# Two transformer blocks on one core: stack loads behind a store, four places for two small tiles, and additions moved from GpSimd to VectorE

## The chip, the cores and the metric

The kernel runs on one NeuronCore of a Trainium2 chip. The metric is device time in microseconds (us), the median of three runs; less is better. A profile of one more execution is read beside it. The engines are called PE (TensorE), DVE (VectorE), ACT (ScalarE), POOL (GpSimd) and SP (SyncE, which here only issues DMAs).

## The reference

16 sequences of 256 tokens with 512 channels pass two blocks. Everything is float32.

```python
# block 0: cross attention to a context, then an MLP with a hidden width of 2048
x = x + mha(ln(x), ln(ctx), mask) @ proj_w + proj_b
x = x + gelu(ln(x) @ fc1_w + fc1_b) @ fc2_w + fc2_b
# block 1: causal self attention, cross attention, a small MLP
mask0 = 1 - all(x == 0)
x1 = ln1(x  + mha1(x, x, mask0, causal=True))
mask1 = 1 - all(x1 == 0)
x2 = ln2(x1 + mha2(x1, ctx, mask1))
z = relu(x2 @ fc1_w.T + fc1_b) * mask0
out = ln3(x2 + (z @ fc2_w.T + fc2_b) * mask0)

# in block 1's attention, 16 heads of 32 channels:
energy  = Q @ K.T                                # Q, K, V times the row mask
lengths = sum(energy[:, :, 0, :] != 0, axis=-1)  # of the first query's row
energy  = -inf where column >= lengths; also where column > row, if causal
out     = softmax(energy / sqrt(32)) @ V
```

## The kernel before

A matrix product in float32 is made of three passes over operands split into a high and a low part (`mm3`). The work goes by groups of two sequences (512 tokens), eight groups in all. Three stages follow one another: block 0's attention (0 to about 780 us of the span), block 0's MLP (to about 1400 us), and block 1 (`block1`). Block 1 has sixteen jobs, eight of self attention and eight of cross attention, and then a small MLP.

**Two streams in each attention.** A generator `stream` makes the attention proper: for each job eight units (two sequences by four chunks of four heads), for each unit four heads with scores (L408), exponentials (L433), transposes (L449) and the product with the values (L468). A generator `feed` makes what a job needs: queries (`project_t` with w["q"]), keys, values, and the transposed inputs of the next job (`front`, `context`). `weave` alternates the two on PE by a running count of cost. Before the first job there is nothing to weave: the first `feed` runs to its end, and only then does the stream build its first unit. PE keeps the order in which the program was written. The instructions of the other engines, and SP's DMA issues with them, are put in order by a planner: it runs a timeline with costs of its own and lets an instruction go when its inputs, its buffer and its engine are free in that timeline. So a DMA that is written late in the program can stand early in SP's queue. Every engine, SP too, then works its queue strictly in order, and an instruction that waits holds up those behind it.

**Stacks.** A chunk of queries or keys (128 rows by 512 tokens, a high and a low part) is taken out of PSUM by ACT and DVE (`split`, L132 and L133; L122 and L123 in block 0) into a tile `qk` and stored to DRAM by `keep` (L378, 512 KB). A unit's operands come back from there into one of three tiles `stack` by `build`: six DMAs of 128 KB (L389, L393), and in block 1 a small one with a row of the length mask (L398). The tile `qk` has one buffer for queries and one for keys in block 0 (`halves`), and two for each in block 1. The next chunk but one (in block 0 the next) cannot be taken out of PSUM before the store of this one has landed.

**Key counts.** For each chunk of keys `lengths` multiplies the first token's queries with the keys (L1280, into a PSUM bank of the tag "pt", of which there are two, shared with the transposes of L449). DVE adds the two parts (L1288, L1289), counts the nonzeros (L1291), makes a row of 0 or -2^100 by a comparison with the tile `cols` (L1296), and SP stores it (L1300). The tiles `lbias` and `n` have two buffers each.

**Context rows.** In cross attention, rows of the context (128 by 512) are loaded into `cx` (`context_rows`, L1435), multiplied by the row mask on POOL (`context`, L1442), transposed on PE (L277) and split. `cx` takes one of three buffers with the tag "t512", which also serve `junk` in `norm` (L1252), and `relu` and `y` in the last MLP. At the end of a job's keys, two or three rows of the next job are asked for; a fourth is asked for once the first has been used.

**Additions and norms.** When a unit is done, `finish` transposes its result (L1347), scales it on DVE into `zz` (L1349), and adds it to the residual `x` on POOL (L1356, 128x256). After every fourth unit two rows' norms are queued (`norm`, `layer_norm`): statistics and scaling on DVE (L238, L239, L241, L251, L252), and one power of -1/2 on POOL (L242).

**Masks.** `tri` (a causal mask of 0 and -2^100, 128x384) and `cols` (the numbers 0 to 255) are made once at the start. `tri` is an operand of the custom DVE instruction of L423, which adds the mask, scales, and takes the minimum in self attention.

Of the kernel before, what the change touches and what calls it, by code (L numbers as in the profile page):

```python
# [10 lines left out]
F32 = mybir.dt.float32  # L11
F32R = mybir.dt.float32r
U8 = mybir.dt.uint8
BF16 = mybir.dt.bfloat16
AF = mybir.ActivationFunctionType
ALU = mybir.AluOpType
# [4 lines left out]
P = 128  # L21
B, S, C, H = 16, 256, 512, 16
D = C // H
HID = 4 * C
KC = C // P
HPC = P // D
NB = 2
NT = S // P
G = NB * NT
N = G * P  # L30
NG = B // NB
EPS = 1e-5
SC = 1.0 / math.sqrt(D)
NEG = -(2.0**100)
# [7 lines left out]
def kernel(ctx: ExitStack, tc: tile.TileContext, a, out):  # L42
# [7 lines left out]
    nc = tc.nc  # L50

    const = ctx.enter_context(tc.tile_pool(name="const", bufs=1))
# [10 lines left out]
    nc.vector.memset(warm, 0.0)  # L63
    nc.scalar.activation(warm, warm, AF.Exp)
    nc.gpsimd.memset(nhalf, -0.5)
    cols = const.tile([P, S], F32, name="cols")
    nc.gpsimd.iota(
        cols, [[1, S]], base=0, channel_multiplier=0, allow_small_or_imprecise_dtypes=True
    )

    tri = const.tile([P, P + S], F32, name="tri")
    nc.gpsimd.memset(tri, 0.0)
    for t, at in ((0, 0), (1, P)):
        w = (t + 1) * P
        nc.gpsimd.affine_select(
            out=tri[:, at : at + w],
            in_=tri[:, at : at + w],
# [9 lines left out]
    for i in range(NB):  # L87
        own = hmask[:, i, i * HPC : (i + 1) * HPC]
        nc.gpsimd.memset(own, 1.0)
        for base, step in ((0, 1), (D - 1, -1)):  # L90
            nc.gpsimd.affine_select(
                out=own,
                in_=own,
# [261 lines left out]
    class Attention:  # L355
# [19 lines left out]
        def keep(self, job, c, slot, t):  # L375

            d = self.scratch.tile([P, 2, N], F32, tag=f"d{slot}", name=f"d{slot}")
            nc.sync.dma_start(out=d, in_=t.bitcast(F32))  # L378
            job.kept[slot, c] = d

        def build(self, job, i, c):
# [98 lines left out]
        def stream(self, jobs):  # L480
            LAG = 3
            heads = [(u, j) for u in range(len(jobs) * len(self.UNITS)) for j in range(HPC)]
            units = {}
            mixed = {}
            for n in range(len(heads) + LAG + 4):
                if n < len(heads):
                    un, j = heads[n]
                    if j == 0:
                        job = jobs[un // len(self.UNITS)]
                        if un % len(self.UNITS) == 0:  # L490
                            yield MARK
                            job.begin()
                        u = units[un] = Unit()
                        u.job = job
                        u.i, u.c = self.UNITS[un % len(self.UNITS)]
                        u.st = self.build(job, u.i, u.c)
                        u.rs = self.pool.tile([P, NT, HPC], F32, tag="rs", name="rs", bufs=3)
                        u.e, u.pt = {}, []
                    self.scores(units[un], j)
                    yield 2 * 110.0  # L500
                if LAG <= n < len(heads) + LAG:
                    un, j = heads[n - LAG]
                    yield self.turn(units[un], j)

                if n in mixed:
                    u = units.pop(mixed.pop(n))
                    yield u.job.finish(u)
                    self.done += 1
                if self.later:
                    self.later.pop(0)()  # L510
                m = n - LAG - 1
                if 0 <= m < len(heads) and heads[m][1] == HPC - 1:
                    mixed[n + 2] = heads[m][0]
                    u = units[heads[m][0]]
                    u.job.scale(u)
                    yield self.mix(u)
            while self.later:
                self.later.pop(0)()
# [4 lines left out]
    class Job:  # L523
        bias = None
# [746 lines left out]
        split_sb(own, (q0[:, :, : NB * HPC], q0[:, :, D:]))  # L1271
        return q0

    def lengths(pool, scratch, k, q0, neg):


        ps = bank("pt", "ps_e0")[: D + NB * HPC, :S]
        for i in range(NB):
            for x in range(2):
                nc.tensor.matmul(  # L1280
                    ps,
                    q0[:, i, :],
                    k[x][:, ts(i, S)],
                    start=(i == 0 and x == 0),
                    stop=(i == NB - 1 and x == 1),
                )
        bias = pool.tile([NB * HPC, S], F32, tag="lbias", name="lbias")
        nc.vector.tensor_copy(bias, ps[D:])  # L1288
        nc.vector.tensor_tensor(bias, bias, ps[: NB * HPC], ALU.add)  # L1289
        n = pool.tile([NB * HPC, 2], F32, tag="n", name="n")  # L1290
        nc.vector.tensor_scalar(  # L1291
            bias, bias, 0.0, None, ALU.not_equal, ALU.add, accum_out=n[:, 0:1]
        )
        nc.vector.reciprocal(n[:, 1:2], n[:, 0:1])
        nc.vector.tensor_scalar(n[:, 1:2], n[:, 1:2], 0.0, neg, ALU.mult, ALU.add)
        nc.vector.tensor_scalar(  # L1296
            bias, cols[: NB * HPC, :], n[:, 0:1], n[:, 1:2], ALU.is_ge, ALU.mult
        )
        d = scratch.tile([NB * HPC, S], F32, tag="dbias", name="dbias")
        nc.sync.dma_start(out=d, in_=bias)  # L1300
        return d


    def block1(mlp0):
        tables, more = {}, {}

        class Mha(Job):
# [11 lines left out]
            def norm(self, t):  # L1319
                x, table = self.x[:, t, :], tables["ln2" if self.cross else "ln1"]  # L1320
                layer_norm(pool, x, table[:, 0, :], table[:, 1, :])
                if not self.cross:
                    junk = pool.tile([P, C], F32, tag="t512", name="junk", bufs=3)
                    nonzero(junk, x, m1[:, self.g, t : t + 1])
                nc.sync.dma_start(
                    out=xd[3 if self.cross else 2][self.g][ts(t, P), :], in_=x
                )
# [16 lines left out]
            def finish(self, u):  # L1344
                pz = u.bank[:, S:].rearrange("p (t n) -> p t n", n=P)
                for t in range(NT):
                    nc.tensor.transpose(pz[:, t, :], u.zs[:, ts(t, P)], ident)  # L1347
                zz = pool.tile([P, NT, P], F32, tag="zz", name="zz")
                nc.vector.tensor_tensor(  # L1349
                    zz.rearrange("p t (j d) -> p t j d", d=D),  # L1350
                    pz.rearrange("p t (j d) -> p t j d", d=D),
                    u.rr.rearrange("p t (j o) -> p t j o", o=1).to_broadcast([P, NT, HPC, D]),
                    ALU.mult,
                )
                xv = self.x[:, u.i * NT : (u.i + 1) * NT, ts(u.c, P)]
                nc.gpsimd.tensor_tensor(out=xv, in0=xv, in1=zz, op=ALU.add)  # L1356
                self.left -= 1
                if self.left % KC == 0:
                    for t in range(u.i * NT, (u.i + 1) * NT):
                        att.later.append(lambda t=t: self.norm(t))  # L1360
                return NT * T_PASS
# [44 lines left out]
        pool = sbuf(ctx, "work3", 2)  # L1406
        scratch = ctx.enter_context(tc.tile_pool(name="scratch3", bufs=10, space=DRAM))
        att = Attention(pool, scratch, 3, True)
        tok0 = [pool.tile([P, NB, D + NB * HPC], F32R, name=f"tok{i}", bufs=1) for i in range(6)]
        for q0 in tok0:  # L1410
            nc.gpsimd.memset(q0.bitcast(F32), 0.0)

        def stage():
            return pool.tile([P, C], F32, tag="pts", name="wst", bufs=6)
# [15 lines left out]
        cxs = {}  # L1430

        def context_rows(n, t):
            if n < len(jobs) and jobs[n].cross and (n, t) not in cxs and t < G:
                cx = cxs[n, t] = pool.tile([P, C], F32, tag="t512", name="cx", bufs=3)
                nc.sync.dma_start(out=cx, in_=of("ctx", jobs[n].g)[:, t, :])  # L1435

        def context(n, t):
# [28 lines left out]
        def feed(n):  # L1466
            job = jobs[n]
# [19 lines left out]

            def count(c):
                job.bias[c] = lengths(
                    pool, scratch, ks.pop(c), q0s[c], -NEG if job.cross else NEG  # L1490
                )
                return 4 * 112.0

# [10 lines left out]
            if n == 0:  # L1504
                weight(0, "v")
            weight(n + 1, "k")
            for t in range(3 if n + 1 > NG else 2):
                context_rows(n + 1, t)
            between = [lambda: count(KC - 1), lambda: following(n, 2)]
            yield from values(pool, w["v"].w, kv, job.v, range(NT), between)  # L1510
# [17 lines left out]
        def up(g, c):  # L1528
            if c == 0:
                h_ts[g] = inputs("c_t")  # L1530
            ps = yield from project_t(w["q"].w, c, x_ts[g])
            r = pool.tile([P, N], F32, tag="t512", name="relu", bufs=3)
            nc.scalar.activation(r, ps, AF.Relu, bias=f1_b[:, c : c + 1])
            split_sb(r, (h_ts[g][0][:, c, :], h_ts[g][1][:, c, :]))

        def down(g, t):
            x = xs[g][:, t, :]
            y = pool.tile([P, C], F32, tag="t512", name="y", bufs=3)
            nc.scalar.activation(y, tables["fc2_b"], AF.Identity, scale=m0[:, g, t : t + 1])
            nc.gpsimd.tensor_tensor(out=x, in0=x, in1=y, op=ALU.add)  # L1540
            ps = yield from project(w["k"].w, h_ts[g], t)
            nc.vector.scalar_tensor_tensor(x, ps, m0[:, g, t : t + 1], x, ALU.mult, ALU.add)
            layer_norm(pool, x, tables["ln3"][:, 0, :], tables["ln3"][:, 1, :])
            nc.sync.dma_start(out=out[NB * g + t // NT, ts(t % NT, P), :], in_=x)
# [83 lines left out]
```

## Time and profile before

| | |
|---|---|
| median of 3 runs | 2765.36 us (2759.30 to 2766.42) |
| the profiled execution's own time | 2762.91 us |
| its span | 2761.2 us |
| PE busy | 2657.0 us, 96% of the span |
| DVE busy | 2051.9 us, 74% |
| ACT busy | 1821.9 us, 66% |
| POOL busy | 630.3 us, 23% |
| granted TensorE clock over the span | 0.991 of full speed |
| self attention, 1440 to 1925 us | PE 474.8 of 485.0 us busy, DVE 359.5, POOL 88.7 |
| cross attention, 1925 to 2600 us | PE 649.3 of 675.0 us busy, DVE 518.5, POOL 161.5 |
| last MLP, 2600 us to the end | PE 152.6 of 161.0 us busy |

The profile is of one execution. A line of it names the source line, the engine, the operation and the tiles, then how long it took; in square brackets stands how long the engine had been idle before it, and what released it. A wait costs time only where the engine that waits is the one that sets the end. "PEclk" is the share of TensorE's full clock that was granted.

### The profile page before, as it was taken

What the parts mean: (1) busy time and instruction counts of PE and PEld (TensorE: products, weight loads), DVE (VectorE), ACT (ScalarE), POOL (GpSimd) and SP (SyncE); (2) the same over time, 40 slices, a digit from 0 to 9 for tenths busy, and PEclk for the clock granted to TensorE, in tenths of its full rate; (3) what the DMA queues carried; (4) which work ended last, traced back from release to release, by engine and by line L of the source; (5) the groups of instructions that cost most, each with busy time, mean ns of one, the idle gap of its engine ahead of it and who ended that gap; (6) DMA issues with size and microseconds to landing.
All of it is one profiled execution on the core that took longest, in us unless ns stands there. A gap on an engine that the chain in (4) does not pass through costs nothing.

```text
span 2761.2 us, 56625 instructions
## 1 busy us (share of the span) xinstructions
PE 2657.0 (96%) x18970; PEld 2241.7 (81%) x18970; DVE 2051.9 (74%) x5947; ACT 1821.9 (66%) x5286; POOL 630.3 (23%) x696
## 2 busy tenths in 40 slices
PE   6999999999899998999989999999999999999998
PEld 5777777776899998999968777777777777777787
DVE  7766667657955569999957777777777777777887
ACT  4877777777655555444547778786777776777522
POOL 6222212113401100111211111115212221214333
PEclk9999999999999999999999999999999999999999
DMA  6655656656333344443464665667565665655321
GB/s 214 197 183 170 182 171 192 182 164 169 107 123 138 123 150 175 168 157 136 167 225 159 195 197 187 194 190 227 183 196 188 188 194 170 189 174 173 97 91 54
DMA packets 287808, 465.40 MB, mean 169 GB/s; under 512 B 36256, under 2 KB 188320, under 8 KB 279328
## 3 DMA queue, kind: packets, MB, share of 16 engines
q1 hardware_dynamic: 287520, 461.78, 52.0%
q8 instruction: 153, 2.51, 0.4%
q14 instruction: 135, 1.11, 0.1%
HBM read 284.97 MB, written 176.69 MB: 167 GB/s over the span
## 4 chain that ended last, share of the span: by engine, by line
PE 76%; DVE 10%; DMA 4%; ACT 3%; issue 3%; POOL 2%; SPq 1%; POOLq 0%; DVEq 0%; ACTq 0%
PE ps_p L258 18%; PE ps_v L258 14%; PE down L1027 9%; PE ps_pt L449 9%; PE ps_z L468 5%; PE ps_s L408 5%; PE up_sc L914 5%; PE up_pt L914 3%; PE up_mm L914 3%; PE ps_t L277 2%; DVE e L423 1%; ACT e L433 1%; DVE x L252 1%; DMA d<-qk 1%; PE ps_z L1347 1%
## 5 line engine op out<-in xcount | busy, mean ns | idle before, releaser
L433 ACT ACTIVATE e<-e,mn 128x256 f32<-128x256 f32 (+1 forms) x1024 | 487.5, 480 | 71.7 <-DVE mn L423 69.4
L455 ACT COPY pt<-ps_pt 128x512 f32<-128x512 f32 (+1 forms) x696 | 378.3, 546 | 178.5 <-PE ps_pt L449 165.5
L449 PE MATMUL ps_pt<-ident,e 128*128 128x128 f32 x2816 | 436.3, 273 | 15.4 <-DVE lbias L1289 8.8
L449 PEld LDWEIGHTS ps_pt<-ident,e 128*128 128x128 f32 x2816 | 336.3, 140 | 56.3 <-DVE lbias L1289 5.7
L408 PE MATMUL ps_s<-stack 97*128 97x256 f32 (+1 forms) x1536 | 331.8, 297 | 18.8 <-ACT e L433 12.0
L408 PEld LDWEIGHTS ps_s<-stack 97*128 97x128 f32 (+1 forms) x1536 | 269.0, 190 | 78.3 <-ACT e L433 19.2
L433 ACT ACTIVATE e<-ps_s,mn 128x256 f32<-128x256 f32 x512 | 240.9, 483 | 59.2 <-DVE mn L419 44.0
L1356 POOL TENSOR_TENSOR x<-x,zz 128x256 f32<-128x256 f32 x128 | 95.4, 745 | 737.0 <-DVE zz L1349 687.0
L1027 PE MATMUL down<-w_h,c_t 128*128 128x256 f32 x900 | 255.4, 285 | 5.6 <-DVE c_t L142 5.6
L1027 PE MATMUL down<-w_h,x_t 128*128 128x256 f32 x868 | 245.9, 283 | 4.4 <-ACT x_t L141 4.4
L423 DVE CUSTOM_DVE_ANT_0 e<-mb,ps_s 128x256 f32<-128x256 bf16 x512 | 192.7, 415 | 75.4 <-PE ps_s L408 73.8
L1027 PE MATMUL down<-w_l,x_t 128*128 128x256 f32 x868 | 246.2, 284 | 0.0
L242 POOL TENSOR_TENSOR rstd<-rstd,nhalf 128x1 f32<-128x1 f32 x192 | 142.4, 747 | 360.6 <-DVE rstd L241 358.8
L258 PE MATMUL ps_p<-x_t,q_h 128*128 128x512 f32 x640 | 215.4, 417 | 4.2 <-DVE qk L128 2.1
L419 DVE TENSOR_REDUCE mn<-ps_s 128x2 f32<-128x512 f32 x256 | 175.1, 684 | 48.7 <-PE ps_s L408 46.5
L468 PE MATMUL ps_z<-pt,v 128*32 128x256 f32 (+1 forms) x3072 | 202.2, 370 | 7.2 <-DVE pt L453 6.5
L423 DVE CUSTOM_DVE_ANT_0 e<-tri,ps_s 128x128 f32<-128x128 f32 (+1 forms) x512 | 160.2, 346 | 53.6 <-PE ps_s L408 51.3
L433 ACT ACTIVATION_READ_ACCUMULATOR e<-e,mn 128x1 f32 x1024 | 197.5, 193 | 0.0
L1027 PEld LDWEIGHTS down<-w_h,c_t 128*128 128x128 f32 x900 | 171.0, 190 | 7.8 <-DVE c_t L142 7.8
L1027 PEld LDWEIGHTS down<-w_h,x_t 128*128 128x128 f32 x868 | 166.4, 192 | 4.8 <-ACT x_t L141 4.6
L468 PEld LDWEIGHTS ps_z<-pt,v 128*32 128x32 f32 x3072 | 83.5, 109 | 105.8 <-issue 28.0
L1027 PEld LDWEIGHTS down<-w_l,x_t 128*128 128x128 f32 x868 | 165.2, 190 | 0.0
(250 smaller groups left out, 7247.8 us busy)
## 6 DMA issues: line engine op xcount, KB each, us to landing
stack<-d SPq DMA_DIRECT2D x1152, 128.0 KB
d<-qk SPq DMA_DIRECT2D x192, 512.0 KB
hid<-ho SPq DMA_DIRECT2D x32, 1024.0 KB
raw<-hid SPq DMA_DIRECT2D x32, 1024.0 KB
x<-xd SPq DMA_DIRECT2D x128, 256.0 KB
xd<-x SPq DMA_DIRECT2D x96, 256.0 KB
xin<-in_x_dram SPq DMA_DIRECT2D x32, 256.0 KB
xin<-in_ctx_dram SPq DMA_DIRECT2D x32, 256.0 KB
```

The lines of the kernel that those rows point to most:

```text
L242: nc.gpsimd.tensor_tensor(out=rstd[:, 1:2], in0=rstd[:, 0:1], in1=nhalf, op=ALU.pow)
L258: nc.tensor.matmul(ps, w[p], x[q], start=(k == 0 and i == 0), stop=(k == kc - 1 and i == 2))
L408: nc.tensor.matmul(ps[:, t, :], u.st[: self.rows, 0, j, ts(t, P)], u.st[: self.rows, 1, j, :], start=True, stop=True,)
L419: nc.vector.tensor_reduce(mn, ps, AX.X, ALU.min)
L423: nc.vector.tensor_tensor_reduce(out=e[:, at], in0=bias[t], in1=ps[:, t, : job.width[t]], scale=-SC, scalar=BIG, op0=ALU.add, op1=ALU.min, ...
L433: nc.scalar.activation(e[:, at], ps[:, t, :] if bias is None else e[:, at], AF.Exp, bias=mn[:, t : t + 1], scale=-1.0, accum_out=u.rs[:, t ...
L449: nc.tensor.transpose(pp[:, ts(x, P)], e[:, at : at + P], ident)
L455: nc.scalar.copy(pt[:, :n], pp[:, :n])
L468: nc.tensor.matmul(z[ts(j, D), w[0] * P :], job.v[u.i * NT + mc][:, u.c * P + j * D : u.c * P + (j + 1) * D], u.pt[j][:, x0 * P : (x0 + le ...
L914: nc.tensor.matmul(ps[:, mm, :], w[p][:, k, :], x[q][:, k, :], start=(first and mm == k == j == 0), stop=(k == 1 and j == 2), skip_group_c ...
L1027: nc.tensor.matmul(ps[:, t, :], x[p][:, mm, ts(t, P)], w[r][:, bo, :], start=(q == mm == t == j == 0), stop=(q == self.NS - 1 and mm == 1 ...
L1356: nc.gpsimd.tensor_tensor(out=xv, in0=xv, in1=zz, op=ALU.add)
```

## The change

It has five edits. (1) `build` of a stream's first unit, and of every later one, is queued on SP behind `first`, the last store that `keep` had issued when the stream began, which is that of the first job's last chunk of keys. Both attentions use `stream`, so this holds for block 0 too. (2) The tag "t512" has four buffers in place of three, and where three context rows of the next job were asked for at the end of the keys, four are. (3) `lbias` and `n` are one tile each over all 128 partitions, and each of a job's four chunks of keys has its own place in it, at partition 0, 32, 64 or 96, in place of two buffers in rotation. (4) In self attention the addition to `x` is made by DVE, in cross attention by POOL as before. (5) `tri` and `cols` are bfloat16, which holds their values exactly; with the smaller `lbias` this frees the SBUF space for the fourth buffer.

```diff
-    cols = const.tile([P, S], F32, name="cols")
+    cols = const.tile([P, S], BF16, name="cols")
...
-    tri = const.tile([P, P + S], F32, name="tri")
+    tri = const.tile([P, P + S], BF16, name="tri")
...
         def keep(self, job, c, slot, t):
             d = self.scratch.tile([P, 2, N], F32, tag=f"d{slot}", name=f"d{slot}")
-            nc.sync.dma_start(out=d, in_=t.bitcast(F32))
+            self.last = nc.sync.dma_start(out=d, in_=t.bitcast(F32)).ins
...
-                        u.st = self.build(job, u.i, u.c)
+                        if un == 0:
+                            first = self.last
+                        with tc.issue_after(first):
+                            u.st = self.build(job, u.i, u.c)
...
-    def lengths(pool, scratch, k, q0, neg):
+    def lengths(pool, scratch, k, q0, neg, place):
...
-        bias = pool.tile([NB * HPC, S], F32, tag="lbias", name="lbias")
+        bias, n, own_cols = (x[place * D : place * D + NB * HPC] for x in (*counts[0], cols))
         nc.vector.tensor_copy(bias, ps[D:])
         nc.vector.tensor_tensor(bias, bias, ps[: NB * HPC], ALU.add)
-        n = pool.tile([NB * HPC, 2], F32, tag="n", name="n")
...
-            bias, cols[: NB * HPC, :], n[:, 0:1], n[:, 1:2], ALU.is_ge, ALU.mult
+            bias, own_cols, n[:, 0:1], n[:, 1:2], ALU.is_ge, ALU.mult
...
+    counts = []
...
-                    junk = pool.tile([P, C], F32, tag="t512", name="junk", bufs=3)
+                    junk = pool.tile([P, C], F32, tag="t512", name="junk", bufs=4)
...
                 xv = self.x[:, u.i * NT : (u.i + 1) * NT, ts(u.c, P)]
-                nc.gpsimd.tensor_tensor(out=xv, in0=xv, in1=zz, op=ALU.add)
+
+                own = nc.gpsimd if self.cross else nc.vector
+                own.tensor_tensor(out=xv, in0=xv, in1=zz, op=ALU.add)
...
+        counts.append(
+            (pool.tile([P, S], F32, name="lbias", bufs=1), pool.tile([P, 2], F32, name="n", bufs=1))
+        )
...
-                cx = cxs[n, t] = pool.tile([P, C], F32, tag="t512", name="cx", bufs=3)
+                cx = cxs[n, t] = pool.tile([P, C], F32, tag="t512", name="cx", bufs=4)
...
                 job.bias[c] = lengths(
-                    pool, scratch, ks.pop(c), q0s[c], -NEG if job.cross else NEG
+                    pool, scratch, ks.pop(c), q0s[c], -NEG if job.cross else NEG, c
                 )
...
-            for t in range(3 if n + 1 > NG else 2):
+            for t in range(G if n + 1 > NG else 2):
                 context_rows(n + 1, t)
...
```

The tiles `relu` and `y` of the last MLP get the same fourth buffer.

More of the change, by code (lines that the diff above doesn't have):

```diff
@@ L1531, in up @@
             ps = yield from project_t(w["q"].w, c, x_ts[g])
-            r = pool.tile([P, N], F32, tag="t512", name="relu", bufs=3)
+            r = pool.tile([P, N], F32, tag="t512", name="relu", bufs=4)
             nc.scalar.activation(r, ps, AF.Relu, bias=f1_b[:, c : c + 1])
@@ L1537, in down @@
             x = xs[g][:, t, :]
-            y = pool.tile([P, C], F32, tag="t512", name="y", bufs=3)
+            y = pool.tile([P, C], F32, tag="t512", name="y", bufs=4)
             nc.scalar.activation(y, tables["fc2_b"], AF.Identity, scale=m0[:, g, t : t + 1])
```

## The prediction

> **What bounds the kernel now.** I read the page first, then the busy time in stretches of 20 us, then the timelines of PE, SP, POOL and DVE around the stretches in which PE loses time. PE is busy 96% of the span and makes most of the chain that ended last:
>
> ```profile
> PE 2657.0 (96%) x18970; PEld 2241.7 (81%) x18970; DVE 2051.9 (74%) x5947; ACT 1821.9 (66%) x5286; POOL 630.3 (23%) x696
> ...
> PE 76%; DVE 10%; DMA 4%; ACT 3%; issue 3%; POOL 2%; SPq 1%; POOLq 0%; DVEq 0%; ACTq 0%
> ```
>
> So an edit gains only where it ends one of PE's waits, and loses where it makes one. No edit touches a matmul. The stretches (PE, PEld, DVE, ACT, POOL, then clock, DMA share, GB/s) show where PE idles in block 1:
>
> ```profile
> 1420.00:1440.00 20.00, 12.57 (x55) 9.85 (x55) 8.66 (x29) 4.89 (x8) 0.00 (x0) 0.74 0.77 252
> 1680.00:1700.00 20.00, 19.11 (x143) 15.37 (x141) 18.87 (x81) 15.82 (x53) 4.14 (x5) 1.00 0.50 160
> 1900.00:1920.00 20.00, 17.29 (x114) 13.07 (x115) 9.79 (x43) 12.36 (x42) 11.27 (x11) 0.91 0.52 144
> 2300.00:2320.00 20.00, 16.55 (x113) 12.29 (x111) 14.05 (x39) 11.76 (x37) 6.61 (x6) 0.91 0.65 202
> ```
>
> 7.4 us are lost at 1420, 2.7 at 1900, 3.5 at 2300, under 1 in a self-attention job's worst stretch (1680), where DVE is nearly full. PE's timeline, in brackets its idle time and the releaser:
>
> ```profile
> 1427.35 0.43 PE L1280 MATMUL ps_e<-qk,tok 128*40 128x256 f32 x1 [6.66 <-ACT qk L132]
> ...
> 1902.39 0.52 PE L449 MATMUL ps_pt<-ident,e 128*128 128x128 f32 x3 [3.05 <-DVE lbias L1289]
> ...
> 1936.11 0.66 PE L277 MATMUL ps_t<-ident,cx 128*128 128x128 f32 x4 [2.19 <-POOL cx L1442]
> ...
> 2313.28 0.61 PE L408 MATMUL ps_s<-stack 97*128 97x256 f32 x2 [2.96 <-ACT e L433]
> ```
>
> **Edit 1, block 1's start.** SP's timeline, first column the start:
>
> ```profile
> 1413.48 0.90 SPq L389 DMA_DIRECT2D stack<-d  x2
> ...
> 1417.45 1.53 SPq L389 DMA_DIRECT2D stack<-d  x2
> 1419.74 0.34 SPq L378 DMA_DIRECT2D d<-qk  x1
> ```
>
> The first key chunk left PSUM at 1410.95 (ACT) to 1412.26 (DVE), but its store went out only at 1419.74, behind stack loads that no one needs before 1437.9, when the first scores run. The third chunk takes the same `qk` buffer, so ACT waited until 1426.7 and PE 6.66 us. With the stacks behind the last store, the first store goes out between 1413 and 1415; about 0.8 MB of norm tables in broadcast form may still stand before it and move at some 240 GB/s, or 3 us. It lands between 1417 and 1421. PE needs the chunk at 1420.7, so its wait falls to 0 to 1.5 us. Behind a wait the clock is low too: the 12 matmuls of the next value tile took 4.25 us, those after it 2.79, so 1.5 us more. The gain is 8.4 at most (6.66 + 0.29 before the next matmul + 1.5), and 4 if the other stores crowd in; I take 7. What is late next: the first unit's seven loads go out behind the last store (about 1422 to 1425.5) and land by 1428 to 1430, against scores that PE would reach at 1429 to 1431. This covers them; if not, they cost what they are late.
>
> **Edit 1, block 0's start.** The same line moves six loads here, and here they are not late now:
>
> ```profile
> 69.58 0.34 SPq L378 DMA_DIRECT2D d<-qk  x1
> ...
> 70.28 0.48 PE L408 MATMUL ps_s<-stack 96*128 96x256 f32 x2
> ```
>
> The last key store went out at 69.58 and the first scores ran at 70.28 without a wait. Six issues of 0.43 us behind the store end at 72.6, and data lands 2.8 us after issue (a store of 65.08 had landed at 68.0): 75, or 4.7 us late, plus 1.5 for the clock. Against that, the store of the second query chunk, issued at 39.51 behind three such loads, landed after 6.5 us where others took 2.8 to 3.3, and PE waited 1.89 and 0.73 us in its chain; 1.5 to 3.3 us come back. Net a loss of 1 to 6.5; I take 3.5. [...]
>
> **Edit 3, key counts.** At 1900.84 DVE's L1288 had waited 1.54 us for an earlier store to leave `lbias`; that goes, with about 1 us of low clock (0.58 from 1904 to 1908). DVE's waits for that store come to 6.2 us in five places. PE's other waits for L1289 (0.15 to 0.88 us, 5.8 together) end mostly on DVE's order, not on the store, and stay. Gain 1.5 to 6, taken 2.5. Four places need that writes to different partitions of one tile do not wait for each other; the stack's six loads do just that, two in 0.90 us.
>
> **Edit 2, context rows.** The fourth row of the first cross job was asked for at 1931.19, when `junk` left its buffer, and PE waited 2.19 us (0.52 at 2013): with a fourth buffer it loads some 6 us sooner. Gain 2.7. In the later cross jobs a chain ends on PE: POOL waits for the fourth row, the norm's power stands behind it, DVE's L252 waits for the power with the next score's minimum behind it, then ACT, then PE:
>
> ```profile
> 2307.53 1.57 POOL L1442 TENSOR_SCALAR cx<-cx,m 128x512 f32<-128x512 f32 x1 [7.84 <-DMA cx<-in_ctx_dram]
> 2309.07 1.07 POOL L242 TENSOR_TENSOR rstd<-rstd,nhalf 128x1 f32<-128x1 f32 x2
> ```
>
> This costs 1.89, 2.96, 0.65 and 1.39 us in four jobs, 0.29 in six, and 1.8 of low clock at 2300: 10.4 together. With four buffers the fourth row is there a job earlier, but the buffer that comes free at this point now takes a row of the job after, which may stand before the power just as well. 0 to 10.4; I take 4, as that row is written later in the program and loads for the stacks go first (before, such a row went out at 2304.88, the fourth at 2301.55).
>
> **Edit 4, additions.** 64 of the 128 go to DVE. No row shows one; the nearest is `zz`, 128x256 too:
>
> ```profile
> L1349 DVE TENSOR_TENSOR zz<-ps_z,rr x128: 393/424/427, 1452.9 to 2596.7; 128x256 f32<-128x256 f32 x128
> L1356 POOL TENSOR_TENSOR x<-x,zz x128: 721/732/1177, 1453.4 to 2598.2; 128x256 f32<-128x256 f32 x128
> ```
>
> 64 x 0.42 = 27 us on DVE, which has 125 us idle of 485 in self attention; so most is hidden by PE. On the path lies what falls into the full stretches (DVE 18.9 of 20): about three additions in each of seven, 21 x 0.42 = 8.8 us at most. DVE's waits for POOL's additions (3.9 us, 10 times) come back, so the least is a gain of 1. I take a loss of 2.5. Two SBUF inputs on DVE can also stall against POOL: L1335 took 1.16 us, not 0.166, while POOL split a weight. [...]
>
> **Edit 5** costs nothing: L423 takes 0.41 us with the float32 `tri` and 0.415 with block 0's bfloat16 `mb`. The buffers in the last MLP lie where PE is full.
>
> **Sum.** 7 - 3.5 + 2.5 + 2.7 + 4 - 2.5 = 10.2 us. The profiled execution took 2762.9 (span 2761.2 and 1.7 around it), so 2752.7; the median lies 2.5 above it, so 2755.
>
> **Rivals.** *The gains are handed back:* the next job's row takes the fourth's place before the power (0, not 4), block 0 loses 6 and block 1 gains 6. 6 - 6 + 2.5 + 2.7 + 0 - 2.5 = 2.7, or 2763. For it speaks that POOL's queue holds the same number of rows. *VectorE becomes the bound in self attention:* the planner puts additions before the scores' minimum, and DVE, at 18.9 of 20 in the full stretches, passes on every addition: 27 us lost, the rest gains 12.7, net 14 slower, 2780. It decides once DVE is at 20 of 20 in stretches such as 1680; against it stand 125 idle us and PE waits under 1 us there now. *The places are not separate:* if a write to one place waits for the store of the last, 64 counts at 0.3 to 1.5 us add 20 to 90; the stack's rows speak against it.
>
> **How the numbers follow.** A measurement of this kernel can tell about 0.3%, 8 us, from no change. The forecast has 0.57, with a range of its own from 2740 (all gains near their upper ends) to 2757. Handed back 0.20, VectorE 0.18, places 0.05. The range from 2740 to 2778 takes in the first two and the near part of the third. Faster 0.57, same 0.20, slower 0.23.
>
> **What would show it.** Right: no wait above 2 us at the last keys near 1420; first scores of block 1 some 7 us earlier, those of block 0 after a wait of 2 to 5 us; no L1288 waiting for a store; POOL's power ahead of a context row. Wrong: PE idle in self attention over 2 us in 20, or DVE at 20 of 20 there; a wait over 8 us at block 0's start; POOL's power still behind a row.

## The result, and the profile after

The change made the kernel slower. The median of six runs is 2785.25 us (2782.24 to 2787.09), against 2763.47 us for the kernel before in the same comparison: ratio 1.0076, 95% interval 1.0063 to 1.0090, or 21.8 us. The prediction was 2755, in a range from 2740 to 2778; the result lies outside it, on the other side of no change. The profiled execution took 2787.1 us; its span is 24.2 us longer than that of before. First the busy times and the chain of waits of the page:

```profile
PE 2664.3 (96%) x18970; PEld 2244.7 (81%) x18970; DVE 2093.8 (75%) x6011; ACT 1825.1 (66%) x5286; POOL 584.5 (21%) x632
...
PE 72%; DVE 15%; DMA 4%; ACT 4%; issue 3%; POOL 1%; SPq 1%; POOLq 0%; ACTq 0%; DVEq 0%
```

VectorE's share of the chain rose from 10% to 15%, PE's fell from 76% to 72%. VectorE is busy 41.9 us more; the 64 additions, at 0.42 us each, account for 27 of it at most, and no other instruction was added. The stretches (PE, PEld, DVE, ACT, POOL, then clock, DMA share, GB/s), which stand some us later in the program than the same stretches of before:

```profile
1420.00:1440.00 20.00, 14.86 (x77) 11.57 (x75) 11.78 (x33) 7.64 (x13) 4.97 (x4) 0.99 0.74 270
1680.00:1700.00 20.00, 18.92 (x150) 14.88 (x149) 17.20 (x70) 15.46 (x52) 1.64 (x2) 1.00 0.63 195
1900.00:1920.00 20.00, 14.86 (x108) 11.09 (x107) 15.86 (x62) 12.44 (x41) 8.93 (x8) 1.00 0.81 222
2300.00:2320.00 20.00, 20.00 (x158) 15.78 (x156) 12.83 (x28) 16.60 (x54) 2.04 (x3) 1.00 0.32 94
```

PE's timeline, in brackets its idle time and the releaser:

```profile
73.15 0.77 PE L408 MATMUL ps_s<-stack 96*128 96x256 f32 x2 [5.76 <-DMA stack<-d]
...
1427.62 0.31 PE L1283 MATMUL ps_e<-qk,tok 128*40 128x256 f32 x1 [1.05 <-ACT qk L132]
...
1440.15 0.76 PE L408 MATMUL ps_s<-stack 97*128 97x256 f32 x2 [3.82 <-DMA dbias<-lbias]
...
1910.81 0.52 PE L449 MATMUL ps_pt<-ident,e 128*128 128x128 f32 x3 [1.73 <-DVE lbias L1292]
...
1944.85 1.09 PE L277 MATMUL ps_t<-ident,cx 128*128 128x128 f32 x4 [3.60 <-POOL cx L1451]
```

Of the large waits that were to go, the one at the last keys did go (6.66 us to 1.05), but 3.82 us came back at the first scores behind it; the wait for the bias fell from 3.05 to 1.73; the one for the context row grew from 2.19 to 3.60. Block 0's first scores, without a wait before, waited 5.76. None of these comes near 22 us. Nor do the prediction's own signs of being wrong show: in stretches of 20 us from 1440 to 1900 PE idles 1.6 us at most and VectorE is at 19.25 at most, and POOL's power stands ahead of the context row (2320.51 and 2325.53). Only from 1900 to 1920, where PE idled 2.7 us before, does it idle 5.1. So the loss lies in no single wait.

As PE's matmuls stand in the same order in both programs, the start of the same matmul can be subtracted, one profile from the other, and this lag shows where the time went. The same was done for the single edits below and for the change without the places; a plus is time lost against the profile of before:

| stage of before (us) | whole change | stacks | rows | places | additions | all but places |
|---|---|---|---|---|---|---|
| 0 to 100 | +3.8 | +4.6 | -0.1 | -0.9 | -1.0 | +4.1 |
| 100 to 1420 | +2.1 | +1.9 | +1.5 | +2.2 | +3.4 | +2.9 |
| 1420 to 1450 | -1.8 | -2.7 | -1.4 | -1.5 | -1.5 | -4.5 |
| 1450 to 1890, self attention | +5.7 | +1.5 | +2.2 | +6.2 | -3.5 | -2.8 |
| 1890 to 2600, cross attention | +11.7 | +1.7 | +3.3 | +14.9 | +2.8 | +2.1 |
| 2600 to the end | +2.7 | 0.0 | +2.7 | -0.1 | 0.0 | +2.7 |
| sum | +24.2 | +7.0 | +8.2 | +20.8 | +0.2 | +4.5 |

The second row shows 1.5 to 3.4 us in every column, also where nothing of that stage was changed, and the third some -1.5 also in the three columns that leave block 1's start as it was: these are differences between two executions, and single figures of this size are not read as effects. The profile of before is of an execution of 2762.9 us, 5 us below the median of the comparison with the single edits (2767.8), so the sums stand some 2 to 7 us above what the ratios give. The ratio of the run in the last column leaves out one execution of 7178.9 us. What stands out is self and cross attention, and there one column is like that of the whole: the four places for key counts.

### The profile page after: what moved, and what is told of

Read it like the earlier page. It is cut to its first block, busy times and chain, and to the rows that moved or that the text cites. A ratio compares the mean times of both kernels' runs of the same rounds, so it can differ in the third digit from the quotient of the medians.

```text
span 2785.4 us, 56624 instructions
## 1 busy us (share of the span) xinstructions
PE 2664.3 (96%) x18970; PEld 2244.7 (81%) x18970; DVE 2093.8 (75%) x6011; ACT 1825.1 (66%) x5286; POOL 584.5 (21%) x632
## 4 chain that ended last, share of the span: by engine, by line
PE 72%; DVE 15%; DMA 4%; ACT 4%; issue 3%; POOL 1%; SPq 1%; POOLq 0%; ACTq 0%; DVEq 0%
PE ps_p L258 17%; PE ps_v L258 13%; PE down L1030 9%; PE ps_pt L449 8%; PE ps_z L468 5%; PE ps_s L408 5%; PE up_sc L917 4%; PE up_pt L917 3%; PE up_mm L917 3%; PE ps_t L277 2%; ACT e L433 2%; DVE e L423 1%; DVE st L238 1%; DVE x L252 1%; DVE mn L419 1%
## 5 line engine op out<-in xcount | busy, mean ns | idle before, releaser
L419 DVE TENSOR_REDUCE mn<-ps_s 128x2 f32<-128x512 f32 x256 | 175.1, 684 | 46.2 <-PE ps_s L408 43.2
L423 DVE CUSTOM_DVE_ANT_0 e<-tri,ps_s 128x128 f32<-128x128 bf16 (+1 forms) x512 | 160.1, 347 | 48.9 <-PE ps_s L408 46.3
L258 PE MATMUL ps_v<-v_h,c_t 128*128 128x512 f32 x384 | 159.2, 423 | 0.0
```

The source lines that it names most:

```text
L258: nc.tensor.matmul(ps, w[p], x[q], start=(k == 0 and i == 0), stop=(k == kc - 1 and i == 2))
L419: nc.vector.tensor_reduce(mn, ps, AX.X, ALU.min)
L423: nc.vector.tensor_tensor_reduce(out=e[:, at], in0=bias[t], in1=ps[:, t, : job.width[t]], scale=-SC, scalar=BIG, op0=ALU.add, op1=ALU.min, ...
```

## The experiments

**The four edits one by one.** The first theory, T1, was that the fourth buffer for context rows, with the order of work that it brought, cost most; T2 was the prediction's own rival, the additions on VectorE; T3 was that any change of order costs. Behind the last key store:

```diff
-            nc.sync.dma_start(out=d, in_=t.bitcast(F32))
+            self.last = nc.sync.dma_start(out=d, in_=t.bitcast(F32)).ins
...
-                        u.st = self.build(job, u.i, u.c)
+                        if un == 0:
+                            first = self.last
+                        with tc.issue_after(first):
+                            u.st = self.build(job, u.i, u.c)
```

> The first stacks behind the last key store, in both blocks, and nothing else of the change. T1 (the whole loses through several small things: two starts that nearly cancel, additions on VectorE, and above all the order of work that the fourth place for context rows brings): block 0's start 4 us later, block 1's last keys 7 to 8 us earlier, of which 4 to 6 are given back at block 1's first scores, so 0 to +3 us against before. T2 (VectorE's additions alone carry the loss): 0 to +3 us too. T3 (no edit carries it, any change of order costs): +5 us or more.

Ratio 1.0003 (0.9993 to 1.0013): no difference, which T1 and T2 allow and T3 does not. Its SP and PE timelines at block 1's start show why the gain at the keys went:

```profile
1429.07 3.65 SPq L378 DMA_DIRECT2D d<-qk  x2
1432.82 1.21 SPq L389 DMA_DIRECT2D stack<-d  x2
...
1436.28 0.29 SPq L398 DMA_DIRECT2D stack<-dbias  x1
```

```profile
1439.35 0.47 PE L408 MATMUL ps_s<-stack 97*128 97x256 f32 x2 [2.33 <-DMA stack<-d]
```

The first line holds two stores. The third chunk's goes out at 1429.07; then SP stands until the last chunk has left PSUM, whose store goes out at 1432.38, and the first unit's loads follow only then. With the low clock behind PE's wait (0.54 of full speed from 1440 to 1444), 5.0 of the 7.7 us gained in the lag are lost again by 1450, and block 0 loses 4.6 in addition.

Four buffers for context rows:

```diff
-                cx = cxs[n, t] = pool.tile([P, C], F32, tag="t512", name="cx", bufs=3)
+                cx = cxs[n, t] = pool.tile([P, C], F32, tag="t512", name="cx", bufs=4)
...
-            for t in range(3 if n + 1 > NG else 2):
+            for t in range(G if n + 1 > NG else 2):
```

> Four places for context rows (with the key counts' columns and the triangle in bfloat16, which make room), and nothing else. T1: the power no longer waits behind a context row, but both scalings then stand ahead of the score minima in every cross job, +1.3 us at each, and in the last MLP three activations stand ahead of the cast, +0.7 us at each of five: +8 to +14 us in all, the largest of the four single edits. T2: 0 to -4 us. T3: about +5 us.

Ratio 1.0012 (1.0001 to 1.0024), some 3 us: much less than T1 wants. What was hoped for did happen: PE's stalls behind the chain from POOL's row fell by 8.4 us in four jobs (2.06 + 3.13 + 0.81 + 1.56, and some 0.85 of low clock behind the longest). But with the power no longer late, VectorE takes both scalings (L252) ahead of the score minimum (L419), in all six jobs. VectorE's and PE's timelines, then PE's of the kernel before at the same scores:

```profile
2313.66 0.69 DVE L252 SCALAR_TENSOR_TENSOR x<-x,rstd,ln 128x512 f32<-128x512 f32 x1
2314.28 0.67 DVE L133 TENSOR_TENSOR c_t<-ps_t,c_t 128x512 fp32r<-128x512 f32 x1
2314.88 0.73 DVE L252 SCALAR_TENSOR_TENSOR x<-x,rstd,ln 128x512 f32<-128x512 f32 x1
...
2315.62 0.67 DVE L419 TENSOR_REDUCE mn<-ps_s 128x2 f32<-128x512 f32 x1
```

```profile
2318.23 0.51 PE L408 MATMUL ps_s<-stack 97*128 97x256 f32 x2 [1.60 <-ACT e L433]
...
2654.44 0.50 PE L258 MATMUL ps_v<-k_h,c_t 128*128 128x512 f32 x1 [0.46 <-DVE x L1542]
```

```profile
2308.68 0.50 PE L408 MATMUL ps_s<-stack 97*128 97x256 f32 x2 [0.29 <-ACT e L433]
```

PE's wait there was 0.29 us before and is 1.60 now: 6 x 1.30 = 7.8 us, most of what was won. (By the lag from 2076 to 2590, which takes in all of the low clock too, 2.2 us are left.) The second line of PE is another cost: the fourth buffer also serves the last MLP, where PE now waits for VectorE in each of five groups. The lag grows by 0.73 us each time and falls a little in between, 2.7 us in all.

The largest single step of this column is neither of the two: from 1898 to 1912, at the turn to cross attention, the lag grows by 5.5 us. There PE waits 3.50 us before a transpose of `e` and 3.77 before the product with the values (3.05 and 0.32 in the kernel before); in the second wait ACT stands until POOL has split a weight (L190), which stands behind a context row on POOL. In the run without the places the same stretch loses 4.4, with the additions alone 2.3, in the whole change 0.2, so whether the fourth buffer is the cause stays open.

Four places for key counts, at partitions 0, 32, 64 and 96 of one tile (with the two tables in bfloat16):

```diff
-        bias = pool.tile([NB * HPC, S], F32, tag="lbias", name="lbias")
+        bias, n, own_cols = (x[place * D : place * D + NB * HPC] for x in (*counts[0], cols))
...
-            bias, cols[: NB * HPC, :], n[:, 0:1], n[:, 1:2], ALU.is_ge, ALU.mult
+            bias, own_cols, n[:, 0:1], n[:, 1:2], ALU.is_ge, ALU.mult
```

> Four places for key counts (and the two tables in bfloat16), nothing else. T1: no count waits for an earlier store, -1 to -3 us; PE's other waits for the last step of a count stay. T2: the same. T3: about +5 us.

Ratio 1.0064 (1.0048 to 1.0080), or 17.7 us, most of what the whole change loses. All three theories missed it. The key to it is VectorE's timeline. In the kernel before, around one step of a count (first column the start, second the duration):

```profile
1628.32 0.40 DVE L423 CUSTOM_DVE_ANT_0 e<-tri,ps_s 128x256 f32<-128x256 f32 x1
1628.66 0.07 DVE L423 DVE_READ_ACCUMULATOR2_ANT mn<- 128x1 f32 x1
1628.66 0.40 DVE L1291 TENSOR_SCALAR_CACHE_REDUCE lbias<-lbias 8x256 f32<-8x256 f32 x1
1629.00 0.07 DVE L1291 DVE_READ_ACCUMULATOR lbias<-lbias 8x1 f32 x1
1629.00 0.15 DVE L1335 TENSOR_TENSOR rr<-rr,m 128x8 f32<-128x8 f32 x1
```

The same step with the four places:

```profile
1631.45 0.41 DVE L423 CUSTOM_DVE_ANT_0 e<-tri,ps_s 128x256 f32<-128x256 bf16 x1
1631.80 0.08 DVE L423 DVE_READ_ACCUMULATOR2_ANT mn<- 128x1 f32 x1
1631.91 0.41 DVE L1290 TENSOR_SCALAR_CACHE_REDUCE lbias<-lbias 8x256 f32<-8x256 f32 x1
1632.26 0.07 DVE L1290 DVE_READ_ACCUMULATOR lbias<-lbias 8x1 f32 x1
1632.36 0.17 DVE L1336 TENSOR_TENSOR rr<-rr,m 128x8 f32<-128x8 f32 x1
```

The durations are the same. But before, each line starts ahead of the end of the one in front (1628.66 + 0.07 = 1628.73, and the next starts at 1628.66); with the places, the count's step starts 0.03 us after its neighbour's end, and the neighbour behind it 0.03 us after the step's. Sorted by place, the medians are plain: at the first place the read of the accumulator is followed 70 ns ahead of its end, as before; at the other three places 31 to 33 ns behind it, and most of the other steps are alike. Where a step uses what the one in front wrote, the gap is there in either kernel (L1291 directly behind L1289: 35 ns), so it is the growth that counts: from 1437 us to the end of the span, the starts with a gap (15 to under 60 ns behind the end in front) grow from 367 to 685. 318 starts that are each some 0.1 us later (31 behind in place of 70 ahead) make an estimated 32 us of VectorE's time. Added up, VectorE's durations have grown by 6 us only (2401.9 to 2407.6); the page's busy time, which counts an overlap once, by 26.7.

Additions on VectorE:

```diff
-                nc.gpsimd.tensor_tensor(out=xv, in0=xv, in1=zz, op=ALU.add)
+                own = nc.gpsimd if self.cross else nc.vector
+                own.tensor_tensor(out=xv, in0=xv, in1=zz, op=ALU.add)
```

> Self attention's additions on VectorE, nothing else. T1: +4 to +7 us, spread over self attention at about 0.8 us for each job, in waits of PE for ACT's casts and for score minima. T2: +14 us or more. T3: about +5 us.

Ratio 0.9991 (0.9979 to 1.0004): no loss, if anything a gain, and self attention is 3.5 us shorter in the lag. T2 falls. The full stretch of self attention and the additions' group:

```profile
1680.00:1700.00 20.00, 19.39 (x154) 15.37 (x152) 19.03 (x84) 15.90 (x54) 2.17 (x2) 1.00 0.56 169
```

```profile
L1357 DVE TENSOR_TENSOR x<-x,zz 128x256 f32<-128x256 f32 x64 | 27.9, 436 | 0.2
```

VectorE does 0.436 us for each, near the 0.42 of the prediction's row, is at 19.03 of 20, and PE is busier (19.39) than before (19.11).

**Is it the partition?** The new theory, T4, which fits these gaps and overlaps (31 to 33 ns at the three places, 70 ns at the first): a VectorE instruction that begins at another partition than its neighbours does not start before they have ended, and the one behind it waits for it in the same way. A rival, T5: four places cost whatever their partitions, since counts run earlier and displace the score minima. Two kernels tell them apart. Four places, all at partition 0:

```diff
-        bias = pool.tile([NB * HPC, S], F32, tag="lbias", name="lbias")
+        bias = pool.tile([NB * HPC, S], F32, tag="lbias", name="lbias", bufs=4)
...
-        n = pool.tile([NB * HPC, 2], F32, tag="n", name="n")
+        n = pool.tile([NB * HPC, 2], F32, tag="n", name="n", bufs=4)
```

> Four places for the key counts, as four tiles that all begin at partition 0, in place of one tile with places at partitions 0, 32, 64 and 96; nothing else (the two tables in bfloat16 make room). T4 (a VectorE instruction that begins at another partition than its neighbours does not start before they have ended): every count instruction starts some 70 ns before its predecessor's end, as the first place's do in the run with the four places alone; no wait for a store; -2 to +2 us against before, so 16 to 20 us better than the run with the four places alone. T3 (any change of order costs): +5 us or more. T5 (four places cost by themselves, since counts run earlier and displace the score minima): +12 to +18 us, as with the four places at 0 to 96. [...]

Ratio 0.9991 (0.9979 to 1.0002); the starts with a gap are 376, near the 367 of before. And two buffers, as before, but every count at partition 32:

```diff
-        bias = pool.tile([NB * HPC, S], F32, tag="lbias", name="lbias")
+        bias = pool.tile([P, S], F32, tag="lbias", name="lbias")[D : D + NB * HPC]
...
-            bias, cols[: NB * HPC, :], n[:, 0:1], n[:, 1:2], ALU.is_ge, ALU.mult
+            bias, cols[D : D + NB * HPC, :], n[:, 0:1], n[:, 1:2], ALU.is_ge, ALU.mult
```

> Two tiles for key counts, as in the kernel before, but used from partition 32 on, all 64 counts; nothing else (the two tables in bfloat16). T4: all count instructions lose the overlap with their neighbours, 64 instead of 48 counts, so 64/48 of what the four places cost, some +20 us, and the waits for the store as before. T3: about +5 us. T5: -2 to +2 us, since the number of places is that of before.

Ratio 1.0091 (1.0076 to 1.0106), 25 us, the slowest of all, with 728 gaps. So the number of places costs nothing that can be measured, and the partition carries the loss: 0, 48 and 64 counts away from partition 0 give 0.9991, 1.0064 and 1.0091. Against the first that is 0.0073 x 2767 / 48 = 0.42 us for a count, and 0.0100 x 2767 / 64 = 0.43: the same price. T5 falls. The VectorE timeline of this kernel shows one thing more:

```profile
1630.23 0.69 DVE L133 TENSOR_TENSOR x_t<-ps_t,x_t 128x512 fp32r<-128x512 f32 x1
1630.95 0.14 DVE L1295 TENSOR_SCALAR n<-n 8x1 f32<-8x1 f32 x1
1631.02 0.40 DVE L1289 TENSOR_TENSOR lbias<-lbias,ps_e 8x256 f32<-8x256 f32 x1
1631.45 0.20 DVE L1334 RECIPROCAL rr<-rs 128x8 f32<-128x8 f32 x1
```

L1295 waits for L133's end (1630.92), and L1334 for L1289's (1631.42); but L1289 starts at 1631.02, ahead of L1295's end (1631.09). In SBUF both of these begin at partition 32. The 64 reads of the accumulator behind their own reduction overlap it there too (median -64 ns). So in these rows it is the change of the first partition between neighbours that costs, not partition 32 itself; the price is an estimated 0.1 us of VectorE's time at each such change (31 ns behind in place of 70 ahead).

**The change without the places:**

```diff
-        bias, n, own_cols = (x[place * D : place * D + NB * HPC] for x in (*counts[0], cols))
+        bias = pool.tile([NB * HPC, S], F32, tag="lbias", name="lbias")
...
+        n = pool.tile([NB * HPC, 2], F32, tag="n", name="n")
```

> The whole change without the four places for key counts: first stacks behind the last key store, four places for context rows, additions on VectorE, bfloat16 tables. T4: the three single edits added up, +1.7 us; -1 to +5. T1 (the fourth context row is what costs in cross attention): +12 us or more. T2: +10 us or more.

Ratio 0.9990 (0.9980 to 1.0000): no loss is left, and T1 and T2 fall once more. T4 had -1 to +5 us; measured are -2.8 (-5.5 to 0.0), so the single edits together are rather better than their sum. The table's last column shows cross attention at +2.1 us in place of +11.7.

**The stacks behind an earlier store, in block 1 alone:**

```diff
+            self.stores.append(nc.sync.dma_start(out=d, in_=t.bitcast(F32)).ins)
...
+                        if un == 0 and self.behind:
+                            first = self.stores[self.behind]
+                        with tc.issue_after(first) if self.behind else nullcontext():
+                            u.st = self.build(job, u.i, u.c)
...
+        att.behind = -2
```

> The first stacks behind the last key store but one, and in block 1 only; nothing else. If block 1's first scores were late because the stacks' loads and the bias row stood behind the fourth store, the 7.7 us gained at the last keys are kept but for 0 to 2, and block 0 loses nothing: -4 to -8 us. If the scores' data is late whatever the order of the queue, -1 to -3 us, as block 1 gained net in the run with this edit alone.

Ratio 0.9984 (0.9974 to 0.9994), some 4 us. Its SP and PE timelines:

```profile
1424.25 0.35 SPq L379 DMA_DIRECT2D d<-qk  x1
1424.70 1.22 SPq L390 DMA_DIRECT2D stack<-d  x2
...
1427.89 0.29 SPq L399 DMA_DIRECT2D stack<-dbias  x1
...
1428.62 0.38 SPq L379 DMA_DIRECT2D d<-qk  x1
```

```profile
1433.87 0.47 PE L409 MATMUL ps_s<-stack 97*128 97x256 f32 x2 [0.49 <-DVE mn L424]
```

The first unit's loads pass ahead of the fourth store, which SP would otherwise stand on, and PE reaches the scores without a wait for data. By the lag 8.0 us are gained at the keys (some 1.5 of them also in the columns that leave block 1's start as it was) and none handed back by 1450: it was the place in the queue.

**What gained, together:** the stacks behind the last key store but one in block 1, the four tiles at partition 0 and the additions on VectorE, with the lines of the three runs:

```diff
+        att.behind = -2
...
+        bias = pool.tile([NB * HPC, S], F32, tag="lbias", name="lbias", bufs=4)
...
+                own = nc.gpsimd if self.cross else nc.vector
+                own.tensor_tensor(out=xv, in0=xv, in1=zz, op=ALU.add)
```

> The three parts that gained or cost nothing alone: first stacks of block 1 behind the last key store but one, four tiles for key counts that all begin at partition 0, self attention's additions on VectorE. If the single gains add up: -4.4 -2.5 -2.5 = -9 us, ratio 0.9966. If they overlap in the same waits: -4 to -6 us.

Ratio 0.9951 (0.9934 to 0.9967): the single gains add up, or more. The gaps lead one step further. In every kernel so far the first step of a count, a copy from PSUM partitions 32 to 39, has a gap of some 31 ns in front, and mostly one of 31 to 34 behind (46 of 64 times in the kernel before). In 16 of the 64 the next instruction there starts some 70 ns ahead of the copy's end; none of these 16 reads PSUM (six are L1252). Moved to ScalarE:

```diff
-        nc.vector.tensor_copy(bias, ps[D:])
+        nc.scalar.copy(bias, ps[D:])
```

> The same, and the copy of the count's second half out of PSUM (it begins at PSUM partition 32, and shows a gap of 31 ns on either side in every kernel so far, where its neighbours overlap by 70) on ScalarE in place of VectorE. T4: this instruction is held as the others are; without it the addition behind it and what stands before it on VectorE follow with an overlap, and VectorE loses 64 x 0.42 us of work and 64 x 0.2 us of gaps; if VectorE's queue still decides in cross attention, -2 to -6 us more than the run with the three parts; if ScalarE's queue (exponentials and casts stand behind the copy) decides, +3 to +10 us.

Ratio 0.9913 (0.9897 to 0.9929), median 2740.55 us against 2764.92: the fastest of all.

```profile
PE 2650.5 (97%) x18970; PEld 2239.1 (82%) x18970; DVE 2044.6 (75%) x5947; ACT 1848.8 (67%) x5350; POOL 588.8 (21%) x632
```

The move brought some 10 us more (0.0038 x 2765), above the 2 to 6 that were expected, and does two things: it takes work from VectorE (busy 2073.5 us with the three parts), and gaps (376 to 303). A last kernel takes the gaps away without moving the work, by leaving the second half out of the count:

```diff
-        nc.vector.tensor_copy(bias, ps[D:])
+        nc.vector.tensor_copy(bias, ps[: NB * HPC])
```

> The run with the three parts, but the count's copy reads the first half's sums (PSUM partitions 0 to 7) in place of the second half's (partitions 32 to 39), so the second half is left out of the count; the instructions are the same in number and kind. It parts what the copy's move to ScalarE brought, 13 us more than the three parts: the 27 us of work that left VectorE, or the gaps around a copy that starts at another PSUM partition. If the gaps alone: the copy overlaps its neighbours by some 70 ns, and the ratio comes near 0.991, -24 us against before. If the work alone: 0.995, as with the three parts. By the price of a held count in the runs with places (0.43 us for some ten gaps, here two), -5 to -7 us against the run with the three parts: 0.993.

Ratio 0.9942 (0.9924 to 0.9960). The copy now overlaps its neighbours (medians of -70 and -71 ns on its two sides at the second and third place), and the starts with a gap are 293, against 376 with the three parts. That the gaps alone bring 0.991 is out; between "some of it" and "none" the interval does not decide, as its runs spread from 2738.8 to 2750.4. How those 10 us divide between work and gaps stays open.

## Why the prediction was wrong, step by step

The single runs answer to the terms of the sum 7 - 3.5 + 2.5 + 2.7 + 4 - 2.5 (a plus is a gain here; key counts and additions by the ratios, the others by the lag or the waits of one profile):

| step | predicted | measured |
|---|---|---|
| block 1's start | +7 | +2.7 (7.7 at the keys, 5.0 back at the scores; some 1.5 also without the edit) |
| block 0's start | -3.5 | -4.6 |
| key counts | +2.5 | -17.7 |
| context rows at 1936 and 2013 | +2.7 | about 0 (-0.6 and +0.8 in the lag) |
| power behind a context row | +4 | +0.6 by the waits (8.4 won, 7.8 lost at the minima), +2.2 by the lag |
| buffers in the last MLP | 0 | -2.7 |
| additions | -2.5 | +2.5 (interval -1 to +6) |

**The step that failed is the key counts.** The prediction asked the right question, whether the places are separate, and answered it from the wrong row. It read from the stack's loads that writes to different partitions do not wait for each other. Those are DMAs; the counts are VectorE instructions. No count of the changed kernel waits for a store (all 9.0 us of L1291's idle time are for PE's sums), so the waits went as the step says; but what it costs a VectorE instruction to begin at another partition, the step put at nothing without a row. In its place the runs showed 17.7 us against before; against four tiles that all begin at partition 0, which cost nothing, it is 0.42 us for each of the 48 counts. The durations would not have told it, since a duration does not hold the overlap with the neighbours. That overlap could be seen in the profile of before, in starts that lie ahead of the last end, and its absence too: the copy out of PSUM partition 32 had a gap of some 31 ns in front there, and mostly one behind. The rival "the places are not separate" had nearly the size (20 to 90 us), but another mechanism, a wait for the store, and a chance of 0.05.

**Block 1's start** was half right. The wait at the keys fell as worked out (6.66 to 1.05, foretold 0 to 1.5). What was late next was named, but its cover was not there: the loads were to go out at 1422 to 1425.5, on the assumption that the last store goes out just ahead of them. It went out at 1432.72 before, and at 1432.38 in the run with this edit alone; as that run was 6.5 us late at 1420, this is 1425.9 in the time of before. So the loads came some 4 us later than foretold, and the scores waited 2.33 for them. **Block 0's start** came as foretold (5.76 us of waiting, 4.7 foretold). **The context row at 1936** was not helped by the buffer: its request waited 0.8 us for `junk` before, but it stands in SP's queue behind the stores of L1325, for which SP waits until the norm is scaled. In the run with the rows alone it goes out at 1937.85, right behind the second of them (1937.44), and PE waits 2.82. **The power behind a context row** did move ahead, and the upper bound of 10.4 us was nearly reached (8.4 by the waits). What the step left out is what the freed power sets going: two scalings of 0.7 us ahead of a minimum for which ACT and then PE wait. **The last MLP** was put at nothing because PE is full there; five waits of 0.46 us came into it. **The additions** were weighed with care and went the other way: VectorE had room for each, so the rival with chance 0.18 falls too; at 19.03 of 20 VectorE was no bound. That this rival's number, 2780, lies near the measured 2785 is chance.

## What to carry to other kernels

On an in-order engine, price an instruction from start to start, with its neighbours, not by its duration (here the durations grew by 6 us and the busy time by 26.7); and give small VectorE tiles their own buffers at partition 0 rather than places at other partitions of one tile, which here cost 17.7 us where four tiles at partition 0 cost nothing that could be measured. At partition 32 the overlap was kept directly behind a neighbour that begins there too (L1289 started 0.07 us ahead of L1295's end). When a load is moved behind a store in a queue, ask how long the queue will stand on that store, and whether an earlier one would do. When a wait is removed, look at what the released work will now stand in front of.

## What the runs showed of the hardware that was not expected

Around the counts, a VectorE instruction that does not use what the one in front wrote mostly started some 70 ns ahead of its end if both began at the same partition, and some 31 ns behind it if not. The same instruction shows it in both forms: with the four places alone, the read of the accumulator of a count is followed at -70 ns at partition 0, at +31 to +33 ns at 32, 64 and 96 (medians). In the whole change the gap behind this read is there in all 48 counts out of place; in the kernel before in 14 of the same 48, 13 of them in front of L1294, which uses what was read. Where an instruction used what the one in front wrote, a gap was there at partition 0 too: L1335 followed L1334, 35 ns behind its end (the median of 69 in the kernel before from 1437 us on). With six or seven such starts in a count (318 for 48), the counts out of place cost 17.7 us of 2765, though VectorE was busy 75% of the span. Part of it is seen where PE's transposes wait for the count to leave a PSUM bank (PE and its weight loads waited 14.5 us for L1289 before, 20.4 with the four places, 11.8 with four tiles at partition 0, but 10.1 with the additions alone, so the figure scatters). How the rest reaches PE was not followed.
